# A depthwise convolution shared between VectorE and ScalarE with adding DMAs, and a layernorm moved forward and folded

## The chip, the cores and the metric

The kernel runs on one core of one Trainium2 chip. The metric is the device time of one execution in microseconds (us); lower is better. All data are 32-bit floats.

## The reference

Eight images of 384 channels and 32x32 positions go through two layers. The first is a transformer block on the 1024 positions of an image as tokens; the second is a convolution block of the ConvNeXt kind, on the first one's output.

```python
# layer 0, for each image, xf: (1024 tokens, 384)
xn = layernorm(xf, g1, beta1)
q, k, v = split(xn @ w_qkv.T + b_qkv)          # 8 heads of 48
out = softmax(q @ k.T * 48 ** -0.5) @ v
x1 = out @ w_proj.T + b_proj + xf
h = gelu(layernorm(x1, g2, beta2) @ w_fc1.T + b_fc1)      # 1536 wide
x = x1 + h @ w_fc2.T + b_fc2
# layer 1
y = depthwise_conv_7x7(x, dw_w) + dw_b         # 49 taps for each channel
y = layernorm_over_channels(y) * ln_w + ln_b
y = gelu(y @ w1 + b1)                          # 1536 wide
gx = sqrt(sum(y ** 2, positions)); nx = gx / (mean(gx) + eps)
y = grn_gamma * (y * nx) + grn_beta + y
out = x + y @ w2 + b2
```

## The kernel before

Channels lie on the 128 partitions, in three tiles (`CT` = 3), and tokens along the free dimension (1024, in two halves of `NH` = 512). So a layernorm over channels has to sum over partitions. It does that with a matmul by a matrix of ones: a sum and then a sum of squares, for each half of the tokens.

The program is one long unrolled list, written out in Python. Each engine runs its own instructions in the order in which they were issued, so the order of issue is the schedule. A planner of some fifty lines, `Flow`, keeps a clock `now` that only matmuls advance (`flow.pe`; `U` = 0.857 us for one matmul of 128x128 by 512 columns, which the trace shows as two records). Side work is written as generators ("chains") that yield how long to pause, in us of that clock; whenever the clock passes a chain's due time, the chain issues its next instructions, which thereby stand between two matmuls. A chain that is `paced` counts from its own due time, others from the clock. `flow.finish(chain)` issues everything that is left of a chain at once. `after(first, chain)` polls once per us of the clock until `first` has been exhausted.

For an image `b` from 1 to 6, TensorE's work stands in this order: `values` (v of the image), `qk`, `attention` (64 steps, in each the scores of one step and the product of the step two before; after half of the steps the first half's projection `proj(b, xt, 0)`), `mlp` (fc1 for token half 0, with the second projection in `rest()` after four of twelve tiles, then fc1 for half 1, then fc2 by a fast product of thirds, `by_thirds`), `grn_up` of the image before, `values` of the next image, and `grn_down` of the image before. The last image goes through `mlp_by_halves` instead.

Beside it run these chains:

- `convolution` (L880): 49 taps for each of three channel tiles, 147 VectorE instructions for one image. Each multiplies a shifted 32x32 window of the padded image `pad` by a per-channel tap and adds it to `acc`. `start_conv` spawns it at the end of `grn_up`, with one instruction each 2.43 us for the first 30 and each 1.8 us after that (1.5 for the last image but one, 1.6 for the first). It covers the image whose MLP has just ended, and so runs under the attention of the next image.
- `layernorm` (L393) with `token_sums` (L367). Without `fold`, the column sums are one matmul of 128x128 ones by 512 columns for each half. With `fold`, an adding DMA on GpSimd's queue first adds one half of the partitions to the other half (64 rows), and two matmuls of 64x64 then suffice for each token half; between the DMA and the matmuls the chain pauses for 3.4 us. `abreast` (L456) runs both token halves in step, with every pause multiplied by `factor`.
- ln1 of the next image runs `abreast` and folded, ln2 of half 0 folded by columns under the attention, ln2 of half 1 unfolded under fc1, and ln3 (the convolution's) `abreast` and unfolded: `next_norms`, called between fc1 and fc2 (`before_fc2`), finishes the convolution and spawns it. `block_differences`, which `grn_up` needs, follows it.
- `average`: four for each half of an attention. Each copies a head pair's output on ScalarE, adds on VectorE, and sends the softmax denominators through small DMAs on SyncE's queue (out, a reciprocal on VectorE, back, broadcast) before a last multiplication on VectorE. The projection needs all four.
- `grn_scale`: twelve ScalarE multiplications of 128x1024, issued between the v tiles and `grn_down`, which multiplies what they make.

GpSimd's queue carries the adding DMAs: those of the folds, two `difference` in fc1 of half 1, and six `adding` in each `by_thirds`. The buffers of tag `res` (three, 128x512) are used in the preparation of weights and at the very end of the program.

Of the kernel before, what the change touches and what calls it, by code (L numbers as in the profile page):

```python
# [46 lines left out]
F32 = mybir.dt.float32  # L47
# [18 lines left out]
NC = HT // CM  # L66
U = 0.857
SCALE = HD ** -0.5
EPS0, EPS1, GRN_EPS = 1e-5, 1e-6, 1e-6
# [81 lines left out]
def block_kernel(  # L151
# [24 lines left out]
    ps_o = ctx.enter_context(tc.tile_pool(name="ps_o", bufs=4, space=PSUM))  # L176
    flow = Flow()
    s_fc2 = dram.tile([P, len(FORMS), 4 * P], F32, tag="s_fc2", bufs=1, name="s_fc2")
    s_w2 = dram.tile([P, len(FORMS), 4 * P], F32, tag="s_w2", bufs=1, name="s_w2")
# [186 lines left out]

    def token_sums(t, name, fold):  # L367

        width = t.shape[-1]
        if fold is None:
            total = o_tile(name)[:, :width]
            nc.tensor.matmul(out=total, lhsT=ones, rhs=t, start=True, stop=True)  # L374
            flow.pe(U * width / NH)
            return [(total, slice(0, width))]
        rows = [slice(0, 64), slice(64, P)]
        parts = [(fold, slice(0, width))]
        if fold == "columns":
            parts = [(j, slice(j * width // 2, (j + 1) * width // 2)) for j in range(2)]  # L380
        for j, cols in parts:
            nc.gpsimd.dma_start(out=t[rows[j], cols], in_=t[rows[1 - j], cols], accum_op=ALU.add)
        yield 3.4
        totals = []
        for j, cols in parts:
            total = o_tile(f"{name}_{j}")[:, : cols.stop - cols.start]
            for i in rows:
                nc.tensor.matmul(out=total[i, :], lhsT=ones[rows[j], :64], rhs=t[rows[j], cols], start=True, stop=True)
            flow.pe(U * width / NH / 2)
            totals.append((total, cols))  # L390
        return totals

    def layernorm(src, dst, h, eps, g, name, switch, spare=None, spaced=False, slow=1.0, fold=None, gentle=False):  # L393

# [15 lines left out]
        yield 2.6 * slow  # L410
        totals = yield from token_sums(a, f"{name}_sum{h}", fold)
        yield 0.8
# [18 lines left out]
        yield 1.8 * slow  # L431
        totals = yield from token_sums(squares[0], f"{name}_var{h}", fold)
        yield 0.8
# [21 lines left out]

    def abreast(*args, places=averages, fold=True, gentle=False, factor=1.4):  # L456

        chains = [
            layernorm(*args[:2], h, *args[2:], spare=places if h else None, fold=h if fold else None, gentle=gentle)
            for h in range(2)  # L460
        ]
        while chains:
            waits = []
            for chain in list(chains):
                wait = next(chain, None)
                if wait is None:
                    chains.remove(chain)
                else:
                    waits.append(wait)
            if waits:  # L470
                yield factor * max(waits)
# [109 lines left out]
    def attention(b, xt, qT, kT, last_tile, first):  # L581
# [44 lines left out]
        for n in range(len(steps) + 2):  # L626
# [4 lines left out]
            if n >= 2:  # L631
                product(*steps[n - 2], ps.pop(n - 2))
            if n - 2 == len(steps) // 2 + 6:
                for chain in first:
# [4 lines left out]
                proj(b, xt, 0)  # L639
                slow = 1.4 if b in (1, B - 1) else 1.0  # L640
                ln = layernorm(xt, xn, 0, eps0, "g2", f"ln2_{b}", False, spaced=True, slow=slow, fold="columns")
                ln = flow.spawn(ln)

        def rest():
            for m in (NP - 1, *range(CT)):
                flow.finish(chains[1, m])
            for seen, op in ((low, ALU.min), (high, ALU.max)):
                ext = small.tile([P, 1], F32, tag="ext", name=f"ext_{b}_{op.name}")
                nc.vector.tensor_reduce(ext, sums, AX.X, op)
                nc.vector.tensor_tensor(seen, seen, ext, op)  # L650
            proj(b, xt, 1)

        return ln, rest, xn
# [63 lines left out]

    def mlp(b, xt, xn, weights, tag, ln, rest, before_fc2):

# [4 lines left out]
        for m in range(HT):  # L724
            gelu_half(hid, m, 0, xn, weights, wa, f"fc1_{b}")
            if m == 3 and rest:
                rest()
                slow = 1.2 if b == 1 else 1.0
                ln = flow.spawn(layernorm(xt, xn, 1, eps0, "g2", f"ln2_{b}", True, slow=slow))
        flow.finish(ln)  # L730
        for m in range(HT):
# [147 lines left out]

    def convolution(acc, us, slow=0, y0=0, y1=H, ready=tuple(range(CT))):  # L880

# [3 lines left out]
        ct, n = None, 0  # L885
        while min(done) < KS * KS:
            left = [c for c in ready if done[c] < KS * KS]
            ct = min([c for c in left if c != ct] or left, key=lambda c: done[c])
# [10 lines left out]
            n += 1  # L899
            yield 2.43 if n <= CT * slow else us  # L900

    def block_differences(acc):
# [77 lines left out]
    def grn_down_straight(b, y, kept, weights, tag, index, todo):  # L980
# [5 lines left out]
        def load():  # L986
            if len(res) < len(todo):
                r, part = todo[len(res)]
                t = three.tile([P, NH], F32, tag="res", name=f"res_{b}_{r}_{part.start}")[:, : part.stop - part.start]
                nc.sync.dma_start(out=t, in_=kept[r * P : (r + 1) * P, part])  # L990
# [164 lines left out]
    def prepare(weights, aside):  # L1155
# [25 lines left out]
        def spare(name):  # L1181
            return three.tile([P, NH], F32, tag="res", name=name)

# [121 lines left out]
    def main():  # L1305
# [40 lines left out]

        state = {"xn": xn, "conv": None, "acc": None, "norm1": None, "norm3": None}
        kept = {}

        def start_conv(b, us, slow=0):  # L1350
            state["acc"] = one.tile([P, CT, N], F32, tag="acc", name=f"acc_{b}")
            state["conv"] = flow.spawn(convolution(state["acc"], us, slow), paced=True)

        def next_norms(b, ln=None):

            if b > 0:
                acc = state["acc"]
                flow.finish(state["conv"])
                norm = abreast(acc, acc, eps1, "lnw", f"ln3_{b - 1}", True, fold=False)
                norm = sequence(norm, block_differences(acc)) if b < B - 1 else after(ln, norm)  # L1360
                state["norm3"] = flow.spawn(norm)
            if b + 1 < B:
# [21 lines left out]
        def last_convolution(h, ct, ln=None):  # L1384
            if ct < 0:
                next_norms(B - 1, ln)
                return
# [8 lines left out]
        for b in range(B):  # L1396
# [6 lines left out]
            if b < B - 1:  # L1403
                mlp(b, xt, xn, weights, b, ln2, rest, lambda: next_norms(b))
            else:
# [5 lines left out]
            if b == 0:  # L1411
                xt = load_x(b + 1, "x")
                flow.finish(preparing)
                start_conv(b, 1.6)
                next_values(1)
# [4 lines left out]
            if b < B - 1:  # L1420
                y, gx = grn_up(b - 1, acc, weights, b - 1)
                start_conv(b, 1.5 if b == B - 2 else 1.8, 10)
                scale = flow.spawn(grn_scale(b - 1, gx, weights, b - 1, y))
                next_values(b + 1)
                flow.finish(scale)
                grn_down(b - 1, y, xt, weights, b - 1, b - 1)
                xt = load_x(b + 1, "x")
            else:
# [34 lines left out]
    def exact_path():  # L1463

        load_wqkv(nc.scalar, nc.scalar)
        with tc.For_i(0, B) as b:
# [10 lines left out]
            ln = layernorm(xt, xn, 1, eps0, "g2", "ln2_x", True)  # L1477
            mlp("x", xt, xn, weights, "x", ln, None, None)
            kept = keep("x", xt)
# [110 lines left out]
```

## Time and profile before

| | |
|---|---|
| time, median of three runs | 3352.0 us (3343.69 to 3355.02) |
| the profiled execution | 3348.34 us, span 3346.6 us, granted clock 0.996 |
| busy share of TensorE, VectorE, ScalarE, GpSimd | 99%, 76%, 42%, 6% |
| one image in the steady part | 404.2 us (matmuls of the query and key begin at 1165.17, 1569.43, 1973.64) |
| DMA | 281.59 MB, 84 GB/s in the mean |
| chain that ended last | PE 87%, DVE 10%, DMA 2%, issue 1% |

The times are those of one profiled execution. The busy share of TensorE is modelled where matmuls overlap, so the chain of waits and TensorE's own list of waits are read beside it. In the rows of groups, one 128x128 matmul by 512 columns is two records.

### The profile page before, as it was taken

How to read it: one execution, taken by the hardware profiler on the slowest of the kernel's cores; microseconds unless marked ns; L12 is line 12 of the kernel's file. 1: busy time of each engine (PE TensorE's matmuls, PEld its weight loads, DVE VectorE, ACT ScalarE, POOL GpSimd, SP SyncE). 2: the span in 40 equal slices, each digit the busy share in tenths (PEclk: the TensorE clock that was granted, in tenths of full speed). 3: DMA queues.
4: the chain of work that ended last, by engine and by line, in shares of the span. 5: the costliest groups of instructions: out<-in, count | busy, mean ns of one | idle time of the engine just before them, and what ended most of it. 6: DMA issues, size and time to landing. Idle time of an engine off the chain costs nothing.

```text
span 3346.6 us, 37477 instructions
## 1 busy us (share of the span) xinstructions
PE 3303.6 (99%) x14282; PEld 1416.7 (42%) x14282; DVE 2550.6 (76%) x3133; ACT 1421.0 (42%) x1884; POOL 208.1 (6%) x243
## 2 busy tenths in 40 slices
PE   8999999999999999999999999999999999999999
PEld 4344434443344433444334443444434444334455
DVE  4344788887877878779797796967888779989950
ACT  3442453444534354352552625426254353522641
POOL 2121000100000000100001000010000110000000
PEclk9999999999999999999999999999999999999999
DMA  5336102642125410445005350062501633023231
GB/s 185 111 105 148 52 20 57 158 102 63 25 70 146 115 47 20 105 122 135 20 16 131 96 140 17 17 157 80 128 18 37 170 83 95 20 56 90 62 98 50
DMA packets 151243, 281.59 MB, mean 84 GB/s; under 512 B 35216, under 2 KB 41232, under 8 KB 150672
## 3 DMA queue, kind: packets, MB, share of 16 engines
q1 hardware_dynamic: 114704, 201.32, 19.6%
q0 software_dynamic: 36064, 77.08, 11.9%
q8 instruction: 115, 1.88, 0.2%
q10 hardware_dynamic: 288, 0.71, 0.1%
q14 instruction: 72, 0.59, 0.1%
HBM read 181.52 MB, written 33.82 MB: 64 GB/s over the span
## 4 chain that ended last, share of the span: by engine, by line
PE 87%; DVE 10%; DMA 2%; issue 1%; ACT 0%; SPq 0%; POOL 0%; DVEq 0%; POOLq 0%
PE o L612 12%; PE s L592 12%; PE fc L345 12%; PE h L352 10%; PE fc_p L352 10%; PE o_p L352 9%; PE qk L332 6%; DVE wqkv L897 4%; PE v L521 4%; PE o L1000 4%; PE proj L535 3%; DVE acc L897 3%; PE h_last L1044 1%; PE qk_last L345 1%; PE ln_var L374 1%
## 5 line engine op out<-in xcount | busy, mean ns | idle before, releaser
L897 DVE SCALAR_TENSOR_TENSOR acc<-pad,vec,acc 128x1024 f32<-128x1024 f32 x1008 | 1230.6, 1276 | 0.0
L601 ACT ACTIVATE p<-s 128x1024 f32<-128x1024 f32 x512 | 523.6, 1024 | 380.6 <-PE s L592 378.4
L592 PE MATMUL s<-qk 48*64 48x512 f32 x4096 | 544.0, 592 | 1.6 <-ACT qk L495 1.5
L612 PE MATMUL o<-p,v 64*64 64x512 f32 x4096 | 538.9, 590 | 0.0
L345 PE MATMUL fc<-xn,fc 128*128 128x512 f32 x1152 | 500.4, 593 | 0.0
L345 PEld LDWEIGHTS fc<-xn,fc 128*128 128x128 f32 x1152 | 218.2, 190 | 278.2 <-issue 268.2
L352 PE MATMUL fc_p<-hid,fc 128*128 128x512 f32 x728 | 318.1, 592 | 0.0
L364 ACT ACTIVATE hid<-fc,bfc_f 128x512 f32<-128x512 f32 x192 | 130.9, 687 | 357.5 <-PE fc L345 357.4
L612 PEld LDWEIGHTS o<-p,v 64*64 64x64 f32 x4096 | 158.6, 133 | 284.6 <-issue 278.1
L592 PEld LDWEIGHTS s<-qk 48*64 48x64 f32 x4096 | 155.5, 133 | 286.0 <-issue 264.3
L945 DVE TENSOR_TENSOR y<-h,y 128x512 f32<-128x512 f32 x288 | 197.2, 690 | 97.8 <-PE h L352 87.3
L352 PE MATMUL o_p<-y,w 128*128 128x512 f32 x624 | 270.9, 592 | 0.0
L352 PEld LDWEIGHTS fc_p<-hid,fc 128*128 128x128 f32 x728 | 138.2, 190 | 174.4 <-issue 170.4
L332 PE MATMUL qk<-xn,wqkv 128*128 128x512 f32 x480 | 207.4, 592 | 0.0
L352 PE MATMUL h<-acc,w_A 128*128 128x512 f32 x432 | 206.4, 596 | 0.0
L897 DVE SCALAR_TENSOR_TENSOR wqkv<-pad,vec,wqkv 128x416 f32<-128x416 f32 (+1 forms) x288 | 193.7, 749 | 0.6
L352 PEld LDWEIGHTS o_p<-y,w 128*128 128x128 f32 x624 | 118.0, 190 | 148.7 <-issue 133.5
L553 DVE TENSOR_TENSOR attn<-o,attn 128x512 f32<-128x512 f32 x64 | 44.1, 689 | 147.2 <-ACT attn L551 147.2
L495 ACT ACTIVATE qk<-qk,bqk 128x1024 f32<-128x1024 f32 x40 | 44.6, 1114 | 229.0 <-PE qk L332 229.0
L712 ACT COPY pad<-x 128x512 f32<-128x512 f32 x48 | 30.2, 635 | 258.3 <-DVE x L777 192.4
L332 PEld LDWEIGHTS qk<-xn,wqkv 128*128 128x128 f32 x480 | 91.1, 190 | 114.1 <-issue 112.0
L535 PE MATMUL proj<-attn,wproj_sb 128*128 128x512 f32 x288 | 129.2, 602 | 2.1 <-DVE attn L579 2.1
(296 smaller groups left out, 3342.5 us busy)
## 6 DMA issues: line engine op xcount, KB each, us to landing
w_A<-in_w SPq DMA_DIRECT2D x72, 384.0 KB, 3.2
fc<-s_fc SPq DMA_DIRECT2D x91, 256.0 KB, 2.8
hid<-hid POOLq DMA_DIRECT2D x42, 512.0 KB, 6.7
fc<-in_wfc SPq DMA_DIRECT2D x54, 384.0 KB, 5.7
w<-s_w SPq DMA_DIRECT2D x78, 256.0 KB, 2.7
y<-y POOLq DMA_DIRECT2D x36, 512.0 KB, 7.0
kept<-x SPq DMA_DIRECT2D x8, 1536.0 KB, 8.3
xn<-in_x SPq DMA_DIRECT2D x14, 768.0 KB, 7.0
```

The lines of the kernel that those rows point to most:

```text
L332: nc.tensor.matmul(out=ps[:, half(h)], lhsT=lhsT(k), rhs=rhs(k)[:, half(h)], start=(k == 0), stop=(k == nk - 1),)
L345: nc.tensor.matmul(out=ps, lhsT=lhsT(k), rhs=rhs(k)[:, half(h)], start=(k == 0), stop=(k == nk - 1))
L352: nc.tensor.matmul(out=bank, lhsT=lhsT, rhs=rhs, start=k == 0, stop=k == len(pairs) - 1)
L364: nc.scalar.activation(dst, src, function, **kw)
L521: nc.tensor.matmul(out=ps[:, :C], lhsT=xn[:, k, t * P : (t + 1) * P], rhs=wv_sb[:, k, :], start=(k == 0), stop=(k == CT - 1),)
L535: nc.tensor.matmul(out=ps, lhsT=wproj_sb[:, m, ct * P : (ct + 1) * P], rhs=attn[:, m, :], start=(m == 0), stop=(m == CT - 1),)
L592: nc.tensor.matmul(out=s[64 * i : 64 * i + 64, j, :], lhsT=kT[64 * j : 64 * j + HD, m, k0 : k0 + 64], rhs=qT[64 * j : 64 * j + HD, m, half ...
L601: nc.scalar.activation(p, s, AF.Exp)
L612: nc.tensor.matmul(out=outs[i][64 * j : 64 * j + 64, :], lhsT=v[keys, t, at : at + 64], rhs=p[keys, j, :], start=(t == 0), stop=(t == KT - 1),
L897: nc.vector.scalar_tensor_tensor(dst, window, tap, dst, ALU.mult, ALU.add)
L945: nc.vector.tensor_tensor(dst, bank, part, ALU.add)
L1000: nc.tensor.matmul(out=ps, lhsT=tiles[k], rhs=y(k, part), start=(k == 0), stop=(k == HT - 1))
```

## The change

Seven of the 49 taps of each channel tile are taken from VectorE. A second chain, `help_convolution`, makes each product on ScalarE into a `res` buffer (now four of them), one token half at a time, and adds it to `acc` by a DMA on GpSimd's queue: 42 of each for an image, one each 2.7 us, for channel tiles 2, 1, 0 in turn. While a tile is in the helper's hands (`taken`, to 8 us beyond its last addition), the convolution leaves it alone. The helper rests while a list `quiet` has an entry: from nine steps ahead of the end of each half of an attention until the projection after it, and during `grn_down`. It goes on 3 us later. The convolutions of images 0 to 6 are helped; the last one, which runs by parts, is not.

ln3 is now spawned behind ln2 of half 1 (`conv_norm`, called in `mlp` right after `rest()` and the spawn of that ln2; in the last image together with `next_norms`, one tile of fc1 after `rest()`), starts when that, the helper and the convolution have ended, and is folded, with pauses of 5.0 us (times 1.4) between DMA and matmul; for the last convolution but one, in the last image, 3.4 us and all pauses times 2.4. `next_norms` finishes helper and convolution as before. ln2 of half 0 pauses for 6.0 us in place of 3.4. Three paces change: the first convolution 1.6 to 1.65, the last but one 1.5 to 1.8, and ln2's `slow` in images 1 and 7 from 1.4 to 1.2.

```diff
+HELPED = 7
...
-        yield 3.4
+        yield wait
...
+            if n - 2 in (len(steps) // 2 - 9, len(steps) - 9):
+                quiet.append("averages")
...
                 proj(b, xt, 0)
-                slow = 1.4 if b in (1, B - 1) else 1.0
-                ln = layernorm(xt, xn, 0, eps0, "g2", f"ln2_{b}", False, spaced=True, slow=slow, fold="columns")
+                quiet.clear()
+                slow = 1.2 if b in (1, B - 1) else 1.0
+                ln = layernorm(xt, xn, 0, eps0, "g2", f"ln2_{b}", False, spaced=True, slow=slow, fold="columns", wait=6.0)
...
             proj(b, xt, 1)
+            quiet.clear()
...
                 ln = flow.spawn(layernorm(xt, xn, 1, eps0, "g2", f"ln2_{b}", True, slow=slow))
+                behind_ln(ln)
...
-        while min(done) < KS * KS:
-            left = [c for c in ready if done[c] < KS * KS]
+        taps = KS * KS - (HELPED if taken is not None else 0)
+        while min(done) < taps:
+            left = [c for c in ready if done[c] < taps and not (taken and taken.get(c, 0) > flow.now)]
+            if not left:
+                yield 1.0
+                continue
...
+    def help_convolution(acc, us, taken):
+
+        yield 8.0
+        for ct in reversed(range(CT)):
+            taken[ct] = float("inf")
+            for i in range(KS * KS - HELPED, KS * KS):
+                dy, dx = divmod(i, KS)
+                for h in range(2):
+                    if quiet:
+                        while quiet:
+                            yield 1.0
+                        yield 3.0
+                    t = three.tile([P, NH], F32, tag="res", bufs=4, name=f"tap_{ct}_{i}_{h}")
+                    y0 = dy + h * H // 2
+                    window = pad[:, ct, y0 : y0 + H // 2, dx : dx + W]
+                    tap = col("dww", ct * KS * KS + i)
+                    nc.scalar.mul(t.rearrange("p (h w) -> p h w", w=W), window, tap)
+                    nc.gpsimd.dma_start(out=acc[:, ct, half(h)], in_=t, accum_op=ALU.add)
+                    yield us
+            taken[ct] = flow.now + 8.0
+        yield 8.0
+        taken.clear()
...
         def start_conv(b, us, slow=0):
-            state["acc"] = one.tile([P, CT, N], F32, tag="acc", name=f"acc_{b}")
-            state["conv"] = flow.spawn(convolution(state["acc"], us, slow), paced=True)
-
-        def next_norms(b, ln=None):
+            acc = state["acc"] = one.tile([P, CT, N], F32, tag="acc", name=f"acc_{b}")
+            taken = {}
+            state["conv"] = flow.spawn(convolution(acc, us, slow, taken=taken), paced=True)
+            state["help"] = flow.spawn(help_convolution(acc, 2.7, taken), paced=True)
+
+        def conv_norm(b, ln):

             if b > 0:
                 acc = state["acc"]
+                how = dict(wait=5.0) if b < B - 1 else dict(wait=3.4, factor=2.4)
+                norm = abreast(acc, acc, eps1, "lnw", f"ln3_{b - 1}", True, **how)
+                if b < B - 1:
+                    norm = sequence(norm, block_differences(acc))
+                state["norm3"] = flow.spawn(after(ln, after(state["help"], after(state["conv"], norm))))
+
+        def next_norms(b):
+
+            if b > 0:
+                flow.finish(state["help"])
                 flow.finish(state["conv"])
-                norm = abreast(acc, acc, eps1, "lnw", f"ln3_{b - 1}", True, fold=False)
-                norm = sequence(norm, block_differences(acc)) if b < B - 1 else after(ln, norm)
-                state["norm3"] = flow.spawn(norm)
...
-                start_conv(b, 1.6)
+                start_conv(b, 1.65)
...
-                start_conv(b, 1.5 if b == B - 2 else 1.8, 10)
+                start_conv(b, 1.8, 10)
...
                 flow.finish(scale)
+                quiet.append("w2")
                 grn_down(b - 1, y, xt, weights, b - 1, b - 1)
+                quiet.clear()
```

## The prediction

> **What bounds the kernel now.** I read the page's busy shares first, then the steady images one by one, then the chain of waits inside one of them, and last TensorE's own list of waits in the stretches that differ. TensorE is busy 99% by the page, but overlapped matmuls make that figure soft, so I take the chain as the witness. Busy time by stretch, one image a line (us, then PE, PEld, DVE, ACT, POOL busy with instruction counts, granted clock, DMA share, GB/s):
>
> ```profile
> 1165.00:1569.00 404.00, 403.63 (x1743) 169.23 (x1742) 325.82 (x378) 178.25 (x222) 23.35 (x22) 1.00 0.33 82
> 1569.00:1974.00 405.00, 404.63 (x1746) 169.52 (x1745) 326.78 (x380) 178.24 (x222) 23.34 (x22) 1.00 0.32 82
> ```
>
> And the chain of waits from fc1 half 1 of an image to its grn_up (start, us, what):
>
> ```profile
> 1751.00 41.20 PE fc L345 x96
> 1792.20 4.29 PE fc_p L352 x10
> 1796.49 1.72 PE ln_sum L374 x4
> 1798.20 8.58 PE fc_p L352 x20
> 1806.79 1.72 PE ln_var L374 x4
> 1808.51 38.62 PE fc_p L352 x90
> 1847.13 6.87 PE h L352 x16
> 1854.00 1.02 PE ln_sum L388 x8
> ```
>
> Every piece starts where the last ended: the steady part is one unbroken run of matmuls, and only two things shorten it: fewer of them, or removing a wait. In an image of 404.2 us TensorE waits 0.4 us (0.2 on qk, 0.2 on ln2's variance). VectorE at 81% and the convolution are hidden there. The lines also hold a price: ln3's unfolded sums take 1.72 us per call (four records), ln1's folded ones 1.02 us (eight). Where the kernel does wait, TensorE's list says so, for image 1 (440 to 560 us) and the last image (2870 to 3030, then to 3170):
>
> ```profile
> PE proj L535 <- DVE attn L579: 2.1, 1, 2.1
> PE ln_var L388 <- DMA ln_sq<-ln_sq: 1.2, 1, 1.2
> PE ln_var L374 <- DVE ln_sq L430: 0.5, 1, 0.5
> ...
> PE ln_var L374 <- DVE ln_sq L430: 5.9, 1, 5.9
> PE ln_sum L374 <- DVE ln_a L409: 2.4, 1, 2.4
> PE ln_var L388 <- DMA ln_sq<-ln_sq: 0.6, 1, 0.6
> ```
>
> **What the skill says.** TensorEngine Tiling (Array Packing), Key Properties: tiles run independently, and changing the tiling mode drains TensorE. The trace agrees: 1.02 us for a folded call against 0.86 us for four 64x64 matmuls side by side, so some 0.16 us goes at the change. ScalarE: Activation LUTs, What ACT_TABLE_LOAD costs: an ACTIVATE with one per-partition pointer operand takes 280 ns + 0.833 ns per column, 706 ns for 512; here a gelu with a bias pointer takes 687 ns and the copy into pad 635. DMA: Bandwidth & Descriptors, Anatomy of one DMA: about 2.0 us fixed plus bytes/436e9, so an estimate of 2.6 us for 256 KB and 3.2 for 512 KB; the trace has 5.2 us for fc_e's 512 KB and 4.5 for 128 KB adding DMAs, and the measurement decides. The same page's rules make an accumulating DMA wait for an earlier one on the same bytes; that matters below.
>
> **The change, part by part.** Times are against the span of 3346.6 us, 5.4 below the median run.
>
> *ln3 folded.* 2 x 1.72 = 3.44 us of TensorE becomes 2 x 1.02 = 2.04, so -1.40 us (-1.72 if nothing drains). It falls on the critical run in images 1 to 6: 6 x 1.40 = **-8.4** (to -10.3).
>
> *VectorE relieved.* 7 convolutions x 21 instructions x 1.276 us = 188 us less on VectorE. In the steady part it is hidden work and worth only the 0.2 us wait of ln2's variance, which comes from three convolution instructions (3.59 us) in front of it: 5 x 0.2 = **-1.0**. In image 1 waits of 3.8 us lie in that crowd. The 1.2 is met by the longer pause (6.0), the 0.5 by a convolution that has run dry by then; of the 2.1 I count half, since the pace there stays (1.65 for 1.6): **-2.8** (0 to -3.8).
>
> *ScalarE's multiplications and their adding DMAs.* 294 of 0.69 us (0.64 to 0.71). Walking the pauses from the start of an image's v: 3 pieces before grn_down, 27 after it through qk and into the attention, 10 after the first projection, the last 2 after the second. Three places could cost.
> (a) At grn_scale ScalarE is the tight engine: the twelfth of its 1.13 us multiplications starts 14.2 us after the first, and grn_down's matmul on tile 7 starts about when that is ready. Of three added pieces the first falls into 1.7 us of idle, the other two into gaps while waiting for v; about 0.2 us comes out the far end. 6 x 0.2 = **+1.2** (0 to 1.3 each).
> (b) In attention a step is 1.72 us and its exponential 1.02; two score banks leave 2.57 - 1.02 less a little, about 1.4 us, before TensorE waits. The worst run is ln2's three squares (0.62, leaving 0.1 a step) with a piece each 2.7 us and a head's copy of 0.58: a lag of about 1.1 us. **0** (to +0.5 an image).
> (c) A piece needs a free res buffer, that is, the DMA four pieces (10.8 us) before landed, and a DMA needs the one two before it on the same half of acc landed, 5.4 us earlier. From fc_e's 5.2 us at 512 KB I take 3.9 us for 256 KB (2.6 to 6): it holds. What waits behind a late one: on GpSimd's queue the fold of ln2, on ScalarE the exponentials. **0** here; it is the rival below. SyncE's small softmax DMAs share the engines, but rest periods of 15 steps (26 us) clear them before each projection; VectorE may lose a microsecond at a reciprocal, hidden by what it was relieved of.
>
> *ln3 moved.* Channel tile 0 comes free about 17 us after the second projection; its seven remaining taps at 1.8 us end 13 us later, and ln3 starts some 31 us after the projection, in fc1 half 1 (which runs from 22 to 54 us), where VectorE idles now. Its first fold queues on GpSimd behind the first fc_e (1773.56 to 1774.8 in the steady image above, 36 us after the projection), so both folds land at 41 to 42.5 us and the sums stand at 41 to 44: 0.2 us x 5 = **+1.0** (0 to 1.5 each). The second fold lies ahead of fc2's adding DMAs; its logarithm comes just behind the last gelu, so no table is loaded twice. ln1 and grn_up stand behind ample pauses.
>
> *The last image.* Before, waits of 2.4 and 0.6 us come from convolution instructions between the proj additions; those run out now. But the helper rests until the second projection and is finished by force 2.6 us later, so the last two pieces and seven taps of tile 0 (7 x 1.28 = 9 us) come in a lump ahead of ln2's subtractions: ScalarE 1.4, GpSimd 1.1 and landing 3.9 put the taps at 9 to 18 us after the projection, subtraction, squares and sums to 23.5, where the variance matmul stands at 18.2: +5.3. The wait of 5.9 us goes, but from 2988 to 3156 us VectorE is solid and TensorE reaches gmean only 0.4 us too early, so that gain is not cashed, nor the seventh fold. -3.0 + 5.3, less something for fewer instructions ahead of gmean: **+1** (-4 to +5).
>
> Sum: -8.4 - 1.0 - 2.8 + 1.2 + 1.0 + 0 + 1 = **-9 us**; 3346.6 becomes 3337.6 on the profiled execution, 3352 becomes **3343** on the median. The runs before spread from 3343.69 to 3355.02, so about 0.3%, 10 us, is what a measurement of this kernel can tell from no change; the likeliest outcome sits at that edge.
>
> **The cases.**
> *A (0.60): hidden, as summed.* Own range -18 to -1; a bit over half of it beyond 10 us.
> *B (0.14): the ends pay too.* Image 1 gives all 3.8 us, and the lump in the last image is smaller than I think, so 3 to 8 us come back there. For it: those waits all name VectorE. Against: VectorE is solid after 2988. -12 - 10 = -22, 3330.
> *C (0.18): slower; the adding DMA is too slow for its pace.* Place: attention. If a 256 KB DMA takes as long as grn_down's adding DMAs do now (7.0 us for y) rather than 3.9, each pair takes 7.0 us instead of 5.4, a tile of seven pairs ends 11 us late, the four buffers cover 10.8 - 7.0 = 3.8, and ScalarE stands before a multiplication with exponentials behind it; less 1.4 of slack, 5 to 6 us for one tile of an image in attention. 7 x 5.5 = 38, less 9: +29, 3381. It decides from a landing of 5.4 us. Against it: 7.0 us holds with two 512 KB transfers and weights at a DMA share of 1.1, and attention has a share of about 0.1.
> *D (0.08): the fold's waits eat it.* ln3's sums wait 1.5 us in each image for DMAs queued behind fc_e: 0, 3352.
> That the change doesn't do what it says is hardly a case: ln3's sums must move from L374 to L388 and 147 records must leave L897.
>
> **How the numbers follow.** Faster by over 0.3%: 0.34 of A and 0.13 of B, 0.47. Within 0.3%: 0.26 of A, 0.01 of B, 0.02 of C and 0.06 of D, 0.35. Slower: 0.16 of C and 0.02 of D, 0.18. The time is A's, 3343. The range from 3324 to 3368 takes in A and B nearly whole, D, and C up to 2.3 us lost in an image; most of C (0.14) and a little of B lie outside.
>
> **What would show it.** Right: L897 on acc falls from 1008 to 861 records; ln3's sums appear under L388 with eight records in about 1.0 us; a steady image takes 403 us rather than 404.2; a 256 KB addition lands within 5 us; in the last image ln2's variance waits about 5 us for VectorE. Wrong: a steady image of over 404.2 us, with TensorE waiting for exponentials or for the folds, or ScalarE's list showing waits on the adding DMA; or an end after 2958 us that shrinks by more than 4 us, which would make my account of the last image false.

## The result, and the profile after

The changed kernel takes 3367.25 us in the median of four runs (3366.72 to 3371.01), against 3351.45 for the kernel before beside it: a ratio of 1.0053 (95% interval 1.0034 to 1.0072). It is slower by half a per cent, 16 us, where 9 us less were forecast. Its profiled execution, the slowest of the four, spans 3369.2 us, 22.6 more than that of before, so the traces show some 7 us more than the medians.

Where the time lies shows in the distance from one image's first query and key matmul to the next one's. Up to image 1 the changed trace is 3.3 us later; the helper's first product comes only at 346.1 us, near the end of that stretch, and over the twelve traces of this study image 1 starts anywhere between 348.5 and 355.6 us. Image 1 takes 408.2 for 410.8 us (-2.6), images 2 to 6 together 2038.3 for 2021.1 (**+17.1**), and from the last image's query and key to the end 569.6 for 564.7 (**+4.8**).

Busy time in the second of the two steady stretches shown for before (us; PE, PEld, DVE, ACT, POOL busy with counts; clock; DMA share; GB/s):

```profile
1569.00:1974.00 405.00, 402.47 (x1744) 167.62 (x1743) 299.87 (x354) 202.46 (x264) 62.34 (x68) 1.00 0.49 108
```

The work was shifted as the prediction says: VectorE is 27 us an image lighter, ScalarE 24 heavier, the DMA share rises from a third to a half. But TensorE, formerly short of the stretch by 0.4 us, is now short by 2.5. Its list of waits over images 2 to 6 (850 to 2760 us) and over the last image (from 2850 us on) names the places:

```profile
PE proj L539 <- DVE attn L583: 13.7, 5, 4.2
...
PE h L334 <- ACT h L1012: 4.9, 1, 4.9
PE fc L347 <- DVE xn L419: 2.9, 1, 2.9
PE ln_var L376 <- DVE ln_sq L433: 2.7, 2, 1.8
```

Before, no projection in images 2 to 6 waited. Now the second projection of every one does, for VectorE's last multiplication of the softmax: 4.2, 3.3, 2.3, 2.4 and 1.5 us. The chain of waits through image 2 (892 to 939 us), which before was matmuls all the way to the projection, has left TensorE (start, us, what):

```profile
895.76 5.01 DMA r<-back
...
900.99 0.69 DVE attn L583
...
905.27 1.99 DVE xn L447 x3
907.26 0.60 DVE attn L557
...
928.21 0.70 DVE attn L583
928.95 8.89 PE proj L539 x14
```

Read it from the bottom: the projection waits for the last head pair's multiplication; that one, through its denominators' round trip, for the third pair's addition (L557), which stood on VectorE behind three multiplications of ln2 (L447) and, in the lines left out, three convolution instructions, all of them behind a broadcast of `r` that took 5.0 us. None of this was on the path before.

### The profile page after: what moved, and what is told of

It is laid out like the page before. It is cut to its first block, busy times and chain, and to the rows that moved or that the text cites. A ratio compares the mean times of both kernels' runs of the same rounds, so it can differ in the third digit from the quotient of the medians.

```text
span 3369.2 us, 38506 instructions
## 1 busy us (share of the span) xinstructions
PE 3312.1 (98%) x14338; PEld 1418.7 (42%) x14338; DVE 2387.5 (71%) x2986; ACT 1593.9 (47%) x2180; POOL 481.3 (14%) x565
## 4 chain that ended last, share of the span: by engine, by line
PE 76%; DVE 7%; issue 3%; DMA 2%; SPq 1%; ACT 1%; POOL 0%; DVEq 0%; ACTq 0%; POOLq 0%
PE h L354 10%; PE fc_p L354 10%; PE s L596 9%; PE o_p L354 9%; PE o L616 9%; PE fc L347 9%; PE qk L334 5%; PE o L1036 4%; PE v L525 3%; DVE wqkv L910 3%; PE proj L539 3%; DVE acc L910 2%; PE h_last L1080 2%; DMA r<-back 1%; PE qk_last L347 1%
## 5 line engine op out<-in xcount | busy, mean ns | idle before, releaser
L910 DVE SCALAR_TENSOR_TENSOR acc<-pad,vec,acc 128x1024 f32<-128x1024 f32 x861 | 1061.5, 1275 | 33.5 <-DMA acc<-tap 30.1
L932 POOL DMA_DIRECT2D acc<-tap x294 | 256.4, 877 | 1186.9 <-ACT tap L931 748.1
L931 ACT ACTIVATE tap<-pad,vec 128x512 f32<-128x512 f32 x294 | 210.6, 726 | 0.1
L539 PE MATMUL proj<-attn,wproj_sb 128*128 128x512 f32 x288 | 133.0, 614 | 16.2 <-DVE attn L583 16.2
```

Source lines behind the costliest of these rows:

```text
L539: nc.tensor.matmul(out=ps, lhsT=wproj_sb[:, m, ct * P : (ct + 1) * P], rhs=attn[:, m, :], start=(m == 0), stop=(m == CT - 1),)
L910: nc.vector.scalar_tensor_tensor(dst, window, tap, dst, ALU.mult, ALU.add)
L931: nc.scalar.mul(t.rearrange("p (h w) -> p h w", w=W), window, tap)
L932: nc.gpsimd.dma_start(out=acc[:, ct, half(h)], in_=t, accum_op=ALU.add)
```

## The experiments

Four theories, numbered as in the expectations: (1) the adding DMAs slow the small softmax DMAs; (2) the longer pause of ln2 (6.0 for 3.4 us) displaces its multiplications; (3) ScalarE's products make its copy of a head late; and, formed after the first four runs, (4) **order of issue**: VectorE takes its instructions in order, and the pause moved 2.1 us of work from ahead of a DMA wait to behind it. The first two then are two halves of one cause. For the last image the question is what its lump costs. Results first. "Images 2 to 6" and "end" are differences from before (us), of one profiled execution each; "projections" is what TensorE waits for projections in the whole execution; "last" is when the multiplication that the second projection needs starts, in us from the image's first query and key matmul, in the mean of images 2 to 6. Before it is 160.4; the projection begins at 161.4, and its first four records take 1.9 us, so that it waits if "last" and its 0.7 us go beyond 163.3: VectorE has a slack of 2.2 us there.

| kernel | ratio (95%) | images 2 to 6 | end | projections | last |
|---|---|---|---|---|---|
| the change | 1.0053 (1.0034 to 1.0072) | +17.1 | +4.8 | 16.2 | 165.3 |
| rest earlier | 1.0023 (1.0012 to 1.0033) | +6.1 | +7.0 | 6.9 | 163.6 |
| short pause | 1.0032 (1.0021 to 1.0043) | +4.7 | +8.2 | 0.9 | 162.6 |
| no adding DMAs | 1.0003 (0.9994 to 1.0011) | +3.8 | -2.4 | 4.7 | 163.3 |
| last but one unhelped | 1.0049 (1.0032 to 1.0065) | +15.0 | +1.5 | 15.6 | 165.2 |
| pause alone | 1.0004 (0.9995 to 1.0012) | +7.6 | -1.1 | 4.3 | 163.2 |
| help alone | 1.0030 (1.0021 to 1.0040) | +5.0 | +5.5 | 0.5 | 162.7 |
| fold alone | 0.9982 (0.9974 to 0.9990) | -4.7 | 0.0 | 1.4 | 160.3 |
| three amendments | 0.9982 (0.9975 to 0.9988) | -0.7 | -1.4 | none | 160.4 |
| convolution rests | 1.0003 (0.9994 to 1.0011) | -2.9 | +6.0 | 2.3 | 162.6 |
| first one helped | 0.9977 (0.9968 to 0.9986) | -3.1 | +0.4 | none | 160.3 |

Before has projection waits of 2.1 us, all in image 1; of the change's 16.2, image 1 has 2.4.

The column "last" sorts the kernels by two things: the long pause, and additions in flight while `r` is broadcast. With neither it stands where it was, at 160.3 to 160.4; with the additions alone (short pause, help alone) at 162.6 to 162.7; with the pause alone (pause alone, no adding DMAs, rest earlier) at 163.2 to 163.6; with both (the change, last but one unhelped) at 165.2 to 165.3. The delays of 2.2 and 2.8 us add up. Each by itself about uses up the slack of 2.2; together they overrun it by 2.7. Where the convolution rests, some of the sum is taken back.

Where an experiment names a time in image 2, it is that of its own trace; the image begins at 760.7 us before, 761.4 in the change, 760.4 with the short pause, 758.1 with the pause alone and 760.1 where the convolution rests.

**Rest earlier.** The helper rests 17 steps instead of nine ahead of the second half's end.

```diff
-            if n - 2 in (len(steps) // 2 - 9, len(steps) - 9):
+            if n - 2 in (len(steps) // 2 - 9, len(steps) - (17 if b < B - 1 else 9)):
```

> In the second half of an attention the helper rests from 17 steps before the end (after 35 of its 42 pieces) instead of 9, in images 1 to 6; nothing else changes. Theory 1 (the helper's adding DMAs delay the softmax broadcast r of the second half, VectorE stands at that multiplication, and the heads behind it reach the projection late): the 5.1 us wait for r falls to about 2 us as before, the projection waits of 2 to 4 us in images 2 to 6 (13.7 us in all) and the clock dips after them (4 us) go; some 16 us less than the changed kernel, near 3350. Theory 2 (the longer pause of ln2 puts 2 us of its multiplications ahead of the third head): the projection still waits, 3365. Theory 3 (ScalarE's pieces make the head's copy late): the projection waits fall too, but the wait for r stays.

Measured: 3358.76 us. The wait for `r` in image 2 falls from 5.1 to 3.5 us, in images 3 to 6 from between 3.1 and 4.8 to about 1.9, and the projections' waits from 16.2 to 6.9. New, the fast product of fc2 waits six times for its own additions, 4.6 us in all: ln3 has slid from fc1 into fc2. So traffic is part of the cause, not all: "last" comes back by 1.7 of its 4.9 us.

**Short pause.** ln2 of half 0 goes back to 3.4 us.

```diff
-..., fold="columns", wait=6.0)
+..., fold="columns")
```

> ln2 of half 0 pauses 3.4 us again in place of 6.0; all else as in the changed kernel. Theory 2 (the longer pause moves ln2's last multiplications ahead of the third head): the projection waits of images 2 to 6 go, 3350. Theory 1 (delayed broadcasts): ln2's 2 us leave the late stretch, so a wait of 4 becomes 2 and one of 2 vanishes, but VectorE still stands 5 us for r; about 3358, and ln2's own folds may now be waited for by TensorE.

Measured: 3359.5 us. VectorE in image 2:

```profile
893.31 2.08 DVE L447 SCALAR_TENSOR_TENSOR xn<-xn,vec,ln_rstd 128x512 f32<-128x512 f32 x3 [0.24 <-ACT ln_rstd L444]
...
897.05 0.69 DVE L583 TENSOR_TENSOR attn<-attn,r 128x512 f32<-128x512 f32 x1 [0.47 <-DMA r<-back]
...
902.08 0.69 DVE L557 TENSOR_TENSOR attn<-o,attn 128x512 f32<-128x512 f32 x1 [0.75 <-ACT attn L555]
```

ln2's multiplications (L447) stand ahead of the multiplication by `r` again and fill its wait, and the third pair's addition (L557) starts 141.7 us into the image, for 145.8 in the change. But TensorE now comes to the fold's sums before the DMA has landed:

```profile
PE ln_var L390 <- DMA ln_sq<-ln_sq: 4.3, 5, 1.1
```

About 0.9 us in each of five images: this is the wait that the longer pause covered. Before, the two folds of ln2's squares landed in 2.5 us and a pause of 3.4 was enough; here, beside the helper's additions on the same queue, they take 3.5.

**No adding DMAs.** ScalarE makes the products; nothing adds them.

```diff
-                    nc.gpsimd.dma_start(out=acc[:, ct, half(h)], in_=t, accum_op=ALU.add)
```

> The adding DMAs of the helper are left out, so seven taps of each tile are multiplied on ScalarE and never added; all else as in the changed kernel. Theory 1 (delayed broadcasts): no projection waits in images 2 to 6, and the lump in the last image is shorter by the landing of 4 us; 3346. Theory 3 (ScalarE's pieces): the projection waits stay, 3362. Theory 2 (longer pause): they stay as well.

Measured: 3348.75 us, level with the kernel before: without the DMAs and with the long pause, the loss is all but gone, so ScalarE's pieces as such cost nothing that can be seen, and theory 3 falls: "last" is 163.3, and 163.2 in pause alone, which has no such pieces. The projections still wait 4.7 us, for the pause is there: VectorE waits for `r` 3.5 us in image 2 and 1.9 in each later one.

**Last but one unhelped.**

```diff
+            if b == B - 2:
+                state["conv"] = flow.spawn(convolution(acc, 1.5, slow), paced=True)
+                state["help"] = None
+                return
```

> The convolution of the last image but one is not helped and has its old pace of 1.5 us; the earlier six are helped as in the changed kernel. If the lump of the last two pieces and seven taps after the second projection of the last image costs what its waits say (2.9 + 1.8 us, and a wait for VectorE passed on to the end): 5 us less than the changed kernel, 3362, all of it after the query and key matmuls of the last image. If the folded and stretched ln3 of the last image is to blame instead: unchanged, 3367.

Measured: 3365.87 us. The end is 3.3 us shorter than after the change, and the rest is as slow as there. By time this kernel and the change are not told apart; in the traces the lump shows, and is small. Over all traces the end bears this out: the change and the four experiments that help the last convolution but one with its DMAs end 4.8 to 8.2 us later than before, the other six between 2.4 earlier and 1.5 later.

**Pause alone**, on the kernel before.

```diff
-                ln = layernorm(..., slow=slow, fold="columns")
+                ln = layernorm(..., slow=slow, fold="columns", wait=6.0)
```

> The kernel before with one number changed: ln2 of half 0 pauses 6.0 us in place of 3.4; no helper, nothing moved. Theory 4 (the pause by itself moves ln2's three last multiplications, 2.1 us of VectorE, from the time in which VectorE stands for the broadcast r anyway to behind that wait, and the third and fourth head are late by as much): VectorE waits some 3.5 us at r where it waited under 1, and the projection waits 1 to 2 us in each image; 3348 becomes 3356 or so. Theory 1 (the adding DMAs alone): no projection waits, 3347, ln2's short wait of 1.2 us in image 1 gone.

Measured: 3351.37 us, no difference by time, where theory 4 had said 3356. Its trace has the displaced order all the same (image 2):

```profile
896.07 0.69 DVE L579 TENSOR_TENSOR attn<-attn,r 128x512 f32<-128x512 f32 x1 [3.81 <-DMA r<-back]
...
900.26 2.07 DVE L444 SCALAR_TENSOR_TENSOR xn<-xn,vec,ln_rstd 128x512 f32<-128x512 f32 x3
902.25 0.69 DVE L553 TENSOR_TENSOR attn<-o,attn 128x512 f32<-128x512 f32 x1
```

It waits at the multiplication by `r`, since ln2 is no longer ahead of it, and the addition comes at 144.2 for 139.8. Image 2 is the worst, though: in images 3 to 5 the wait is 1.8 to 1.9 us and the addition comes at 142.2 to 142.3. In image 2 the last piece of `r` took 3.9 us, with none of the helper's additions in flight, as it took 3.6 with no adding DMAs and with rest earlier, against about 2 in their other images. In all three traces a packet of the instruction queue (0.9 us) starts in that stretch, 135.7 to 135.8 us into image 2, but one at 135.6 us in image 3 of no adding DMAs delays nothing, so what holds `r` up there stays open. The 5.0 us of `r` in image 2 of the change need not be the additions' work alone. In the mean "last" is 2.8 us late with the pause alone, just past the slack of 2.2; the traffic adds 2.1 more, nearly all of which the projections pay.

**Help alone.** Short pause, ln3 unfolded and where it was before.

```diff
-                norm = abreast(acc, acc, eps1, "lnw", f"ln3_{b - 1}", True, **how)
...
+                norm = abreast(acc, acc, eps1, "lnw", f"ln3_{b - 1}", True, fold=False)
```

> Helper as in the changed kernel, ln2's pause 3.4 us again, ln3 unfolded and behind fc1 as before. Theory 4: no projection waits to speak of; TensorE waits about 0.8 us for ln2's second fold in each image, since that DMA shares the engines with the helper's additions; an image 404.5 to 405.5 us, 3352 to 3360 with the lump in the last image. If the fold and move of ln3 were what costs: 3346.

Measured: 3357.88 us. The projections hardly wait (0.5); the folds of ln2 do, 4.1 us in five images, and the end is 5.5 us later. So the helper costs something by itself, and not by the mechanism of the change's main loss.

**Fold alone.** No helper, paces and pauses of before, ln3 moved and folded.

```diff
-            taken = {}
-            state["conv"] = flow.spawn(convolution(acc, us, slow, taken=taken), paced=True)
-            state["help"] = flow.spawn(help_convolution(acc, 2.7, taken), paced=True)
+            state["conv"] = flow.spawn(convolution(acc, us, slow), paced=True)
```

> No helper, the convolution and its paces as before, ln2's pause 3.4; only ln3 is spawned behind ln2 and the convolution, and folded. Gain by the prediction: 1.4 us in an image of 404.2, unless its folds, which now fall into fc2 beside the adding DMAs of by_thirds, are waited for. No waits: 402.8 an image and 3341; with waits of 1 to 2 us: 404 and 3348. The helper's use for the fold is the difference.

Measured: 3343.07 us, 0.18% faster than before. A steady image takes 403.2 for 404.2 us. In the change the fold earned less. There ln3's sums came one half after the other, here together:

```profile
978.98 1.08 PE L390 MATMUL ln_sum<-ln_a,ones 64*64 64x512 f32 x4
980.01 1.08 PE L390 MATMUL ln_sum<-attn,ones 64*64 64x512 f32 x4
```

```profile
988.84 0.65 PE L390 MATMUL ln_sum<-ln_a,ones 64*64 64x512 f32 x2
988.86 0.65 PE L390 MATMUL ln_sum<-attn,ones 64*64 64x512 f32 x2
```

The first fence is the change (fc1), the second this kernel (fc2), both TensorE in image 2; of the second two more such lines follow, at 989.32 and 989.34. Together the halves share the array and take 1.02 us; one after the other they take 2.03, more than the unfolded 1.72. Both kernels issue these matmuls in the same order; what differs is when the data is there. In the change the two adding DMAs of the fold were issued at 973.15 and 973.68 us, behind one of fc_e at 972.43, and took (KB each, us to landing)

```profile
ln_a<-ln_a POOLq DMA_DIRECT2D x1, 128.0 KB, 5.6
attn<-attn POOLq DMA_DIRECT2D x1, 128.0 KB, 6.2
```

so that they landed at 978.8 and 979.9, and each half's matmuls begin 0.1 to 0.2 us after their own landing. In images 3 to 6 the sums come apart in the same way. Here, with much the same DMAs, TensorE reaches the sums 14 us after the second landing. A longer pause for ln3 in the change was not tried.

**Three amendments**: the edits of rest earlier, short pause and last but one unhelped together.

> The changed kernel with ln2's pause 3.4 us, the helper's rest in the second half from 17 steps before the end, and the last image's convolution unhelped. Theory 4: no projection waits, less of the 0.8 us waits for ln2's second fold, no lump; images 2 to 6 at 403.5 to 404.5 us and 3345 in all. If something else in the helper costs, images stay at 405 and 3354.

Measured: 3342.83 us. No projection waits, and the end is 1.4 us shorter than before. What is left against fold alone is the wait of the fast product for its additions, 4.5 us in six waits in images 2 to 6.

**Convolution rests.** The change as it is, pause of 6.0 and all, but VectorE's convolution instructions keep out from nine steps ahead of the second half's end until the projection. It takes away neither the DMAs nor the pause, only what is queued.

```diff
-                quiet.append("averages")
+                quiet.append("late" if n - 2 > len(steps) // 2 and b < B - 1 else "averages")
...
-            if not left:
+            if not left or (taken is not None and "late" in quiet):
```

> The changed kernel with ln2's pause still 6.0 us and the helper as it is, but the convolution's own VectorE instructions rest too from nine steps before the end of an attention's second half until the projection (images 1 to 6), and are made up for afterwards. Theory 4 (what is late is VectorE's queue: behind the wait for r stand three convolution instructions and ln2's multiplications, and the third and fourth head behind those): with the convolution out of that queue the heads are on time though r lands as late as before; the projection waits (16.2 us) fall below 3 us and images 2 to 6 to 404 to 405 us, some 13 us less, near 3354. If the broadcasts themselves are what comes last, the projection waits stay.

Measured: 3349.32 us, level with the kernel before, and images 2 to 6 are 2.9 us shorter than there. VectorE in image 2:

```profile
905.75 0.68 DVE L557 TENSOR_TENSOR attn<-o,attn 128x512 f32<-128x512 f32 x1
...
924.69 0.69 DVE L583 TENSOR_TENSOR attn<-attn,r 128x512 f32<-128x512 f32 x1 [6.12 <-DMA r<-back]
```

The addition comes as late as in the change (145.7 us into the image for 145.8), for the pause and the DMAs are there; but from it to the last multiplication it is 18.9 us for 21.0. In the mean the addition comes at 144.3 for 144.6 and "last" at 162.6 for 165.3, within the slack. Between 860 and 2600 us VectorE waits 97 us for `r`, for 55 in the change, and the kernel is faster. So the expectation came true by half: the third head is as late as before, and what the rest takes away is queue behind it, which is on the path in the kernel before too (20.5 us from the addition to the last multiplication there, 20.7 in the change, 18.4 here) but was covered by the slack. In image 2 the projection still waits 2.1 us.

**First one helped.** Fold everywhere, short pause and longer rest; only the first convolution, which has image 1's crowd, is helped; the others have the paces of before.

```diff
+            if b > 0:
+                state["conv"] = flow.spawn(convolution(acc, us, slow), paced=True)
+                state["help"] = None
+                return
```

> The parts that measured well put together: ln3 moved and folded everywhere, ln2's pause 3.4 us, only the first convolution helped (with the rest from 17 steps before the end), all other convolutions on VectorE with the paces of the kernel before. By the runs so far: image 1 at 404.4 us as with all three amendments, images 2 to 6 at 403.2 as with the fold alone, the last at 564: 10 us under the kernel before, 3339. If the helped first image hands its lateness on, no better than the fold alone, 3343.

Measured: 3340.43 us, faster than both kernels: 0.9977 of before. Image 1 takes 404.3 us, against 410.8 before and 408.9 with the fold alone, and no projection waits. By the intervals it can't be told from fold alone or from the three amendments.

## Why the prediction was wrong

**The step that failed** is the treatment of VectorE at the end of an attention. Two sentences carry it. "The 1.2 is met by the longer pause (6.0)" entered the pause as a gain in image 1 alone; that every image has this pause, and what it pushes where, was not costed. And part (c) had rest periods of 26 us that "clear them before each projection; VectorE may lose a microsecond at a reciprocal, hidden by what it was relieved of". The helper's last pieces run until those rests, when the third-last broadcast of `r` is under way; and the relief is not there: in this stretch the convolution still issues at its old pace, and VectorE's idle time comes later, after the projection. VectorE in image 2, before and after:

```profile
892.70 2.08 DVE L444 SCALAR_TENSOR_TENSOR xn<-xn,vec,ln_rstd 128x512 f32<-128x512 f32 x3 [0.38 <-ACT ln_rstd L441]
...
895.89 0.69 DVE L579 TENSOR_TENSOR attn<-attn,r 128x512 f32<-128x512 f32 x1
896.49 3.67 DVE L897 SCALAR_TENSOR_TENSOR acc<-pad,vec,acc 128x1024 f32<-128x1024 f32 x3
900.53 0.69 DVE L553 TENSOR_TENSOR attn<-o,attn 128x512 f32<-128x512 f32 x1 [0.37 <-ACT attn L551]
```

```profile
900.99 0.69 DVE L583 TENSOR_TENSOR attn<-attn,r 128x512 f32<-128x512 f32 x1 [5.09 <-DMA r<-back]
901.60 3.67 DVE L910 SCALAR_TENSOR_TENSOR acc<-pad,vec,acc 128x1024 f32<-128x1024 f32 x3
905.19 2.07 DVE L447 SCALAR_TENSOR_TENSOR xn<-xn,vec,ln_rstd 128x512 f32<-128x512 f32 x3
907.18 0.68 DVE L557 TENSOR_TENSOR attn<-o,attn 128x512 f32<-128x512 f32 x1
```

The same instructions stand in both. Before, L444 and a tap ran while `r` was on its way, and VectorE did not wait for it; after, it stands idle for 5.1 us (3.1 to 4.8 in images 3 to 6) and L447 comes on top. The Trainium skill says it in one clause (TensorE: Matmul & The Clock Gate, Architectural detail: the array is 16× 32×32): VectorE is strictly first in, first out. The trace agrees: the last input of L447's three instructions is there at 900.2 us, but they start at 905.2, behind L583 and three taps of which they read nothing. A busy share of VectorE, which fell, could not show this.

The DMA part is measured in the window from 880 to 902 us. Issues there, before and after (KB each, us to landing):

```profile
ln_sq<-ln_sq POOLq DMA_DIRECT2D x2, 64.0 KB, 2.5
...
r<-back SPq DMA_DIRECT2D x2, 32.0 KB, 1.8
```

```profile
acc<-tap POOLq DMA_DIRECT2D x8, 256.0 KB, 4.0
ln_sq<-ln_sq POOLq DMA_DIRECT2D x2, 64.0 KB, 3.9
...
r<-back SPq DMA_DIRECT2D x2, 32.0 KB, 4.1
```

With eight additions issued in these 22 us the small pieces of `r` take 4.1 for 1.8 us (image 2; in images 4 to 6 it is 3.0 to 3.4 for 1.9 to 2.9), and the fold of ln2, which the longer pause was to cover, 3.9 for 2.5. Against the zero of part (c), images 2 to 6 have 13.7 us of projection waits and, by the granted clock, 4.4 us behind them (below); less some 2 for the fold and 1 for ln2's variance makes 15 of the 17.1. About 2 us I could not place.

**The fold**: -1.40 an image was right for the sums where both halves' data is there; the image gave 1.0 when the fold was alone, and in the change the sums took 2.03 and the squares 1.02, 3.05 for 3.44, so 0.4. Rival D named the reason: the folds land one after the other behind fc_e. The list of waits shows 0.5 us of it in five images, but the late second half also cost the sharing of the array, some 1.0 us an image. The term for it ("ln3 moved") was +1.0 for all five images and should have been some +5.

**ln2's variance**: its 0.2 us is gone from images 2 to 6, as predicted. **grn_scale**: +1.2 was not seen; from an image's v to its query and key it is 67.24 us in both traces. **Image 1**: the steps that fall into it sum to -4.0 (fold 1.4, relief 2.8, grn_scale 0.2); it gave 2.6, since waits of 2.4 (projection), 1.4 and 0.3 us (ln2 of half 1, for VectorE) took the place of the old 3.8. That rival B's 3.8 us were to be had shows in the last experiment, where image 1 is 1.1 us longer than a steady image, for 6.6 before.

**ScalarE and the adding DMA** (the slower rival): a product takes 726 ns for 690, the 256 KB addition lands in 3.3 us in the median for 3.9. ScalarE does not run into its buffers, and the exponentials do not wait. C named the right resource, the adding DMAs in attention, and the wrong victim: not ScalarE behind its buffers, but SyncE's small DMAs that VectorE waits for.

**The last image**: the mechanism is as predicted. The seven taps wait 6.0 us for the last landing and run from 2983.3 to 2992.5, 8 to 17 us after the projection (9 to 18 predicted):

```profile
2983.29 9.21 DVE L910 SCALAR_TENSOR_TENSOR acc<-pad,vec,acc 128x1024 f32<-128x1024 f32 x7 [6.00 <-DMA acc<-tap]
2992.42 1.88 DVE L419 SCALAR_TENSOR_TENSOR xn<-ln_sum,x 128x512 f32<-128x512 f32 x3
```

TensorE then waits 2.9 on fc and 1.8 on the variance, 4.7 for 5.3. The size of the sum was off: the 3.0 us of waits that went are not in the end time, which is +4.8 for +1. A wait of 4.9 us for ScalarE's `h` (L1012) stands at 3106 us, where before had none; but the fold alone has it too, with an end of 0.0, so it takes the place of the old 5.9 us and does not explain the +4.8. Why the 3.0 us are lost stays open.

## What to carry to other kernels

An engine that runs in order has a slack at each place of its queue, not a share of busy time: before lengthening a pause or adding traffic, write down the queue between two waits on the path, and see which instructions lie ahead of a wait (free) and which move behind it. A timer that is lengthened to cover one DMA moves everything that follows it, and the same traffic that made it necessary also lengthens the waits that it now lies behind. Take a relief where the queue is crowded, as resting the convolution or helping only the first image did, not on average.

## What the runs showed of the hardware

**The granted clock halves behind some short waits of TensorE.** Around the projection's wait of 4.2 us in image 2 (PE, PEld, DVE, ACT, POOL busy; clock; DMA share; GB/s):

```profile
920.00:925.00 5.00, 4.79 (x11) 1.82 (x10) 4.15 (x6) 1.38 (x2) 0.00 (x0) 1.00 0.07 11
925.00:930.00 5.00, 1.05 (x2) 0.53 (x3) 4.15 (x8) 0.00 (x0) 0.00 (x0) 0.74 0.24 58
930.00:935.00 5.00, 5.00 (x8) 2.05 (x7) 3.88 (x4) 0.00 (x0) 0.00 (x0) 0.57 0.00 0
```

Eight matmul records fit into five us, where 13 did at full clock just after (935 to 940 us). The clock is at half from 927.4 to 934.3 us, so the wait of 4.2 us costs 2.7 more. The wait of 2.3 us in image 4 is followed by 3.4 us at half (1.7 more), that of 3.3 us in image 3 by no dip, so length alone does not decide.

The Trainium skill (TensorE: Matmul & The Clock Gate, What's actually happening) has the clock fall to half after an idle window of about 3.4 us, the window running freely. The traces agree on the window: in each of the twelve, all changes of the clock lie on one grid of 3.41 us (in the change 927.43, 1746.63 and 3105.14 us are among them, 240 and 398 steps apart). They differ on how idle it has to be. Of the wait in image 2, 2.6 us lie in the window that ends at 927.43, and all 2.3 us of image 4 in the one that ends at 1746.63; the 3.3 us of image 3 are cut at 1337.0 into 1.6 and 1.75. From image 1 on, in all twelve traces, a window at full clock in which the profile has TensorE idle for more than 2 us was always followed by half the clock and one with less than 1.6 us idle never; between these, either happened. So a projection's wait of 2 to 4 us in the change costs up to 2.7 us more or nothing, by where it falls on the grid.

**Two folded sums share the array only when the data of both is there**: 1.02 us for the two halves together, 2.03 for the same eight records when the second half's DMA landed 1.1 us after the first's.

**Additions of 256 KB slow small DMAs in the same stretch**: 64 KB on the same queue takes 3.8 to 4.1 us for 2.3 to 2.7 before (images 2 to 6), and 32 KB on SyncE's queue 3.0 to 3.4 us for 1.9 to 2.9 (images 4 to 6).
